# Two attentions on one core: row sums by eight products with ones, held sums, a warmed array, and f and g through seven exp tiles

## The chip, the cores and the metric

The kernel runs on one core of one Trainium2 chip. The metric is the device time in microseconds (us) of a whole execution. The engines are TensorE (PE in the profile; PEld is its weight load), VectorE (DVE), ScalarE (ACT), GpSimd (POOL) and SyncE (SP, which here only issues DMAs). Runs of one kernel agree within 0.14% (the widest spread is that of run 8, 2987.79 to 2991.91 us). All runs below are of the fast state.

A ratio below is the mean time of one kernel's fast runs over that of the other's of the same rounds, so it is not quite the ratio of the medians that are quoted.

## The reference, cut to what matters

Two layers over x of shape 8 x 64 x 64 x 64, that is eight images of 64 channels and 4096 positions:

```python
# layer 0 ("first kind" below)
f = Wf x + bf            # 8 channels
g = Wg x + bg            # 8 channels
h = Wh x + bh            # 64 channels
s = f^T g                # 4096 x 4096 scores of each image
x = x + h softmax(s)^T
# layer 1 ("second kind" below)
xn = group_norm(x)       # 8 groups
q, k, v = Wqkv xn + bqkv
out = Wp (softmax(q k^T / 8) v) + bp + x
```

## The kernel before

The kernel computes exp of the scores without a maximum, multiplies by the values, and divides by the row sums at the end. Each image and kind has four chunks of 512 columns for each half of the positions. Each chunk has 16 steps. A step makes four score banks, takes exp of them into one tile `e` of 128 x 2048, multiplies it with the values (`weigh`), and adds it on VectorE to the chunk's sum tile `esum`. The order is: first kind of image 0, first kind of image 1, second kind of image 0, first kind of image 2, second kind of image 1, and so on. So the run begins with eight chunks of the first kind in a row.

The sum tile has two halves `esum[:, 0]` and `esum[:, 1]`, and what is summed over the 128 partitions is their total. It is closed in one of two ways:

```python
        def holds(self, c):
            return self.kind == 0 and self.b > 0 and c < (1 if self.b == 1 else NC - 1)
...
            def halves():
                if other is not None:
                    vector.tensor_add(raw, raw, other)
                vector.tensor_add(esum[:, 0], esum[:, 0], esum[:, 1])

            def transposed():      # the way of "held" chunks: VectorE sums over partitions
                ...
                vector.tensor_reduce(part, esum[:, 0].rearrange(...), axis=AX.X,
                                     op=ALU.add, apply_transpose=True)
                ...
            def sums(spare):       # the other way: products with ones on TensorE
                for h in range(2):
                    for i in range(2):
                        row = 32 * (2 * h + i)
                        matmul(z[row : row + 32, 0:width], ones[:, 0:32],
                               esum[:, 0, h, ts(i, width)],
                               start=True, stop=True, tile_position=(0, row))
...
        held = at.holds(c)
        if at.kind == 1 or next_kind == 1 or held:
            when = now + 4
            if at.kind == 0:
                when = (i // NC + 1) * NC * NT + 1 + 3 * c     # inside the second kind
            for s, u in ((0, halves), (1, transposed), (5, reciprocals), (8, result)):
                at_step(when + s, behind(u), 0)
            return
        behind(halves)()
        ...
        at_step(now + delay, lambda: sums(spare), BANK)
```

f and g of the first kind are split into a high and a low part through two tiles, `full` and `high`, of which there is one each (`bufs=1` in the pool `work`). The exp tiles come from a pool of six:

```python
    ppool = ctx.enter_context(tc.tile_pool(name="ppool", bufs=6))
...
            full = work.tile([P, 2, CW], F32, tag="full", bufs=1, name=f"full_{n}")
            nc.scalar.activation(full[rows], ps[rows], AF.Identity, bias=fgb[rows, :])
            high = work.tile([P, 2, CW], F32R, tag="high", bufs=1, name=f"high_{n}")
            vector.tensor_copy(high[rows], full[rows])          # the cast
            ...                                                 # subtraction, then DMAs read high
```

Of the kernel before, what the change touches and what calls it, by code (L numbers as in the profile page):

```python
# [9 lines left out]
F32 = mybir.dt.float32  # L10
# [58 lines left out]
def fast_path(  # L69
# [28 lines left out]
    const = ctx.enter_context(tc.tile_pool(name="const", bufs=1))  # L98
    xpool = ctx.enter_context(tc.tile_pool(name="xpool", bufs=3))
    proj = ctx.enter_context(tc.tile_pool(name="proj", bufs=1))  # L100
    ppool = ctx.enter_context(tc.tile_pool(name="ppool", bufs=6))
    work = ctx.enter_context(tc.tile_pool(name="work", bufs=2))
    small = ctx.enter_context(tc.tile_pool(name="small", bufs=2))
    dram = ctx.enter_context(tc.tile_pool(name="dram", bufs=1, space=bass.MemoryType.DRAM))
# [16 lines left out]

    made_last = {}
    added = None
    tight = False

    def in_order(made, engine="tensor"):

# [22 lines left out]
    def matmul(*args, **kwargs):  # L150
        in_order(nc.tensor.matmul(*args, **kwargs))  # L151

    def behind(work_):


        def made():
            with tc.issue_after(added):
                work_()

        return made  # L160
# [22 lines left out]
        return t  # L183


    w1 = const.tile([P, 2, C8], F32, name="w1")
    for i, (w, queue) in enumerate(((WfT, nc.scalar), (WgT, nc.sync))):
        for h in range(2):
# [24 lines left out]
    with tc.issue_after(masked):  # L213
# [10 lines left out]
        wfg = const.tile([P, 2, 4, C8], F32, name="wfg")  # L224
        nc.vector.tensor_copy(wfg, w1.unsqueeze(2).broadcast_to([P, 2, 4, C8]))
    wfg = wfg.rearrange("p i s c -> p (i s c)")
    fgb_low = const.tile([P, 2], F32, name="fgb_low")
    fgb, lowmask = fgb_low[:, 0:1], fgb_low[:, 1:2]
    for j in range(2):
# [20 lines left out]
    nc.vector.tensor_single_scalar(odd, lane, 1, op=ALU.bitwise_and)  # L250
    lowmask32 = const.tile([P, 1], F32, name="lowmask32")
    nc.vector.tensor_scalar(lowmask32, odd, -1.0, None, op0=ALU.mult)
    ones = const.tile([P, C], F32, name="ones")
    nc.vector.memset(ones, 1.0)


    QP = 2 * CW // P
# [67 lines left out]
    class Attention:  # L325
# [7 lines left out]

        def holds(self, c):

            return self.kind == 0 and self.b > 0 and c < (1 if self.b == 1 else NC - 1)

        def values(self, src, w, c):

            ps = pair()  # L340
            for t in range(TPC):
                for m in range(2):
                    for h in range(2):
                        matmul(
                            ps[ts(m, C), h, ts(t, C)], src[ts(h, C), ds(t * P + m * C, C)],
                            w[ts(h, C), :], start=True, stop=True,
                        )

            copy = vector.tensor_copy if self.kind == self.b == c == 0 else nc.scalar.copy
            copy(  # L350
                self.vt[:, :, ts(c, TPC), :],
                ps[:, :, 0 : TPC * C].rearrange("k p (t c) -> k p t c", c=C),
            )

        def finish(self, acc, esum, c, index):

            n = f"{self.name}_{c}"
            raw = work.tile([P, CW], F32, tag="raw", bufs=4, name=f"raw_{n}")
            other = self.total(raw, acc, index)
            zt = small.tile([P, QP], F32, tag="zt", bufs=4, name=f"zt_{n}")  # L360
            width = CW // 2
            r = four = None
# [6 lines that stand above are left out]
            def transposed():  # L369


                nonlocal four
                both_ = work.tile([P, 8 * QP], F32, tag="zs", name=f"part_{n}")
                part = both_[:, 0:32]
                four = both_[:, 32:].rearrange("p (a k) -> p a k", k=QP)
                vector.tensor_reduce(
                    part, esum[:, 0].rearrange("p h (i b) -> p b (h i)", b=32),
                    axis=AX.X, op=ALU.add, apply_transpose=True,
                )
                for a in range(4):  # L380
                    nc.sync.dma_start(four[:, a, :], part[ts(a, 32), :])

            def sums(spare):

                z = banks[:, spare, :]

                zs = work.tile([P, width], F32, tag="zs", name=f"zs_{n}")
                for h in range(2):
                    for i in range(2):
                        row = 32 * (2 * h + i)  # L390
                        matmul(
                            z[row : row + 32, 0:width], ones[:, 0:32], esum[:, 0, h, ts(i, width)],
                            start=True, stop=True, tile_position=(0, row),
                        )
                nc.scalar.copy(zs, z[:, 0:width])
                for h in range(2):
                    for i in range(2):
                        row = 32 * (2 * h + i)
                        nc.sync.dma_start(zt[row : row + 32, :], zs[row : row + 1, :])  # L399

            def broadcast():
                nonlocal r
                r = work.tile([P, CW], F32, tag="r", name=f"r_{n}")

            def reciprocals():
                rt = stash[:, ts(index, QP)]
                if four is not None:
                    vector.tensor_reduce(
                        zt, four.rearrange("p a k -> p k a"), axis=AX.X, op=ALU.add
                    )  # L410
                vector.reciprocal(rt, zt)
                broadcast()
                dealt = recips[index]
                nc.sync.dma_start(dealt, rt)
                for h in range(2):
                    row = dealt[ts(h, C), :].rearrange("p e -> (p e)")
                    nc.sync.dma_start(r[ts(h, C), :], row.partition_broadcast(C))

            def result():
                vector.tensor_mul(raw, raw, r)  # L420
                self.residual(raw, c)

            return halves, transposed, sums, reciprocals, result
# [52 lines left out]
    class Layer0(Attention):  # L476
# [4 lines left out]
        def before(self):  # L481
# [24 lines left out]
                        load_x(b)  # L506

            if self.b == 0:
                return [(-1, begin, True), (0, rest, True)] + [
                    (  # L510
                        (-1, 1, 5, 8)[c],
                        lambda c=c: self.values(x_tiles[0][:, ts(c, CW)], wh, c),
                        True,
                    )
                    for c in range(NC)
                ]
# [16 lines left out]
        def home(self, c):  # L533

            if self.b > 1:
                if c == 0:
                    layers1[self.b].own(F32)
                return layers1[self.b].parts[:, c, :]
            layers0[2].own_vt()
            return layers0[2].vt.rearrange("q p t c -> q (p t c)")  # L540

        def project_direct(self):

            ps = pair()
            full = work.tile([P, 2, CW], F32, tag="full", bufs=1, name="full_direct")
            high = work.tile([P, 2, CW], F32R, tag="high", bufs=1, name="high_direct")
            for i, dst in enumerate((self.f, self.g)):
                matmul(
                    ps[:, i, :], direct[:, i, :], x_tiles[self.b][:, 0:CW], start=True, stop=True
                )  # L550
                nc.scalar.activation(
                    full[:, i, :], ps[:, i, :], AF.Identity, bias=bias2[:, i : i + 1]
                )
                vector.tensor_copy(high[:, i, :], full[:, i, :])
                vector.scalar_tensor_tensor(
                    dst[:, 0:CW], high[:, i, :].bitcast(F32), lowmask2[:, i : i + 1],
                    full[:, i, :], op0=ALU.mult, op1=ALU.add,
                )

        def project(self, k, js=(0, 1)):  # L560
# [4 lines left out]
            for j in js:  # L565
                for h in range(2):
# [1 line left out]
                        ps[ts(j, C), h, :], wfg[ts(h, C), :], xt[ts(h, C), ts(2 * k + j, CW)],  # L568
                        start=True, stop=True,
                    )  # L570
            full = work.tile([P, 2, CW], F32, tag="full", bufs=1, name=f"full_{n}")
            rows = slice(js[0] * C, P)
            nc.scalar.activation(full[rows], ps[rows], AF.Identity, bias=fgb[rows, :])  # L573
            high = work.tile([P, 2, CW], F32R, tag="high", bufs=1, name=f"high_{n}")
            vector.tensor_copy(high[rows], full[rows])

            split = high
# [16 lines left out]
        def project_all(self):  # L594
# [6 lines left out]
            for c in range(NC):  # L601
                for h in range(2):
# [1 line left out]
                        ps[ts(c, 32), h, :], wfg32[ts(h, C), :], xt[ts(h, C), ts(c, CW)],  # L604
                        start=True, stop=True, tile_position=(h * C, 32 * c),
                    )
            full = work.tile([P, 2, CW], F32, tag="full", bufs=1, name=f"full_{n}")
            nc.scalar.activation(full, ps, AF.Identity, bias=fgb32)
            high = work.tile([P, 2, CW], F32R, tag="high", bufs=1, name=f"high_{n}")
            vector.tensor_copy(high, full)  # L610
            split = high
            vector.scalar_tensor_tensor(
# [46 lines left out]
    class Layer1(Attention):  # L659
# [8 lines left out]
        def before(self):  # L668
# [32 lines left out]
            def deviations():  # L701
# [8 lines left out]
                )  # L710
                y = guess.bitcast(F32)
                w = small.tile([P, 1], F32, tag="w", name=f"w_{n}")
                for i in range(4):
                    vector.scalar_tensor_tensor(w, y, y, ve, op0=ALU.mult, op1=ALU.mult)
                    vector.tensor_scalar(w, w, -0.5, 1.5, op0=ALU.mult, op1=ALU.add)
                    vector.tensor_mul(y, y, w)
# [179 lines left out]
    def finished(i, now):  # L896
# [7 lines left out]
        if at.kind == 1 or next_kind == 1 or held:  # L904
# [4 lines left out]
            for s, u in ((0, halves), (1, transposed), (5, reciprocals), (8, result)):  # L909
                at_step(when + s, behind(u), 0)  # L910
            return
        behind(halves)()

        spare = outer[c % 2 if at.kind == 0 else 1]
        delay = 7 if at.kind == 0 else 5
# [499 lines left out]
```

## Time and profile before

| | before |
|---|---|
| median of the first three runs | 3005.96 us |
| span of the profiled run | 3004.0 us |
| TensorE busy | 2973.7 us |
| VectorE busy, 90 to 338 us | 236.46 of 248 us |
| first scores of the second kind start at | 338.95 us |
| one period (one image's first and second kind) after that | 368.5 us |

The prediction shows the lines. The busy time of TensorE is the row to start with: what a change can take out without removing matmul work is the 30 us in which it is idle, and the time that a slow clock adds to its busy time. The busy time doesn't show the second part: the granted clock was 0.75 at 14 to 16 us, 0.50 at 16 to 24 and 0.69 at 24 to 26, as much as some 10 us at 0.50, which by an estimate from these numbers is 5 us of busy time. The second row to look at is the stretch of the eight first chunks, in which VectorE is nearly full as well.

### The profile page before, as it was taken

Reading aid. Unit: us, or ns where it says so; the run is one execution under the profiler, and the core shown is the slowest. Engines: PE = TensorE matmul, PEld = TensorE weight load, DVE = VectorE, ACT = ScalarE, POOL = GpSimd, SP = SyncE. Lnnn points to the kernel's source line nnn. Section 1 sums busy time; section 2 is a strip of 40 time slices with the busy share of each in tenths; the row PEclk is TensorE's granted clock in tenths of the full one; section 3 lists DMA queues with packets and bytes.
Section 4 is the critical chain, followed back from the end, with each engine's and each line's share of the span. In section 5 each row is a group of like instructions: output and inputs, shape, how many; then the busy total and the mean of one; then the engine's idle time right before and its main releaser. Section 6 shows DMA issues by size and latency. Waiting matters only on the chain.

```text
span 3004.0 us, 58286 instructions
## 1 busy us (share of the span) xinstructions
PE 2973.7 (99%) x25629; PEld 1078.7 (36%) x25629; DVE 2574.0 (86%) x1659; ACT 2073.0 (69%) x2019; POOL 16.1 (1%) x40
## 2 busy tenths in 40 slices
PE   8999999999999999999999999999999999999998
PEld 3333333333333333333333333333333333333333
DVE  7999986899878998789986999879997799976776
ACT  6888656786567866678666785668856688566554
POOL 2000000000000000000000000000000000000000
PEclk9999999999999999999999999999999999999999
DMA  2100100101001010010100102000020000000000
GB/s 65 43 8 15 47 16 19 30 1 44 20 20 29 1 45 19 21 28 1 49 19 20 26 1 51 16 23 22 1 52 20 19 8 1 17 24 15 9 16 13
DMA packets 77141, 66.93 MB, mean 22 GB/s; under 512 B 54048, under 2 KB 54080, under 8 KB 75088
## 3 DMA queue, kind: packets, MB, share of 16 engines
q1 hardware_dynamic: 75792, 63.01, 8.7%
q8 instruction: 202, 3.31, 0.5%
q14 instruction: 59, 0.48, 0.1%
q0 software_dynamic: 768, 0.09, 0.0%
q10 hardware_dynamic: 320, 0.04, 0.0%
HBM read 39.84 MB, written 12.32 MB: 17 GB/s over the span
## 4 chain that ended last, share of the span: by engine, by line
PE 93%; DVE 4%; issue 1%; ACT 1%; DMA 0%; SPq 0%; DVEq 0%; ACTq 0%
PE banks L151 93%; DVE esum_l L141 3%; DVE vt_l L141 1%; ACT e_l L1013 1%; DMA x<-in_x_dram 0%; DVE x L141 0%; DVE raw_l L141 0%; DVE st_l L141 0%; ACT full_l L573 0%; DVE high_l L141 0%; DVE kq_l L141 0%; DVE rt L141 0%; SPq L399 0%; DMA zt_l<-zs_l 0%; DVE w_l L141 0%
## 5 line engine op out<-in xcount | busy, mean ns | idle before, releaser
L141 DVE TENSOR_TENSOR esum_l<-esum_l,e_l 128x2048 f32<-128x2048 f32 x629 | 1438.9, 2288 | 272.0 <-ACT e_l L972 246.3
L972 ACT ACTIVATE e_l<-banks 128x1024 f32<-128x1024 f32 x1024 | 992.2, 1022 | 680.6 <-PE banks L151 680.6
L151 PE MATMUL banks<-e_l,v_l 64*64 64x512 f32 (+1 forms) x8780 | 1090.2, 586 | 0.0
L1013 ACT ACTIVATE e_l<-banks 128x2048 f32<-128x2048 f32 (+3 forms) x727 | 953.8, 1373 | 183.5 <-PE banks L151 165.9
L151 PE MATMUL banks<-kq_l 64*64 64x512 f32 (+1 forms) x8448 | 1004.4, 585 | 6.5 <-ACT e_l L1013 5.7
L151 PE MATMUL banks<-e_l,vt_l 128*64 128x512 f32 (+1 forms) x4056 | 829.8, 550 | 0.0
L141 DVE TENSOR_TENSOR kq_l<-kq_l,e_l 128x2048 f32<-128x2048 f32 x252 | 577.5, 2292 | 24.4 <-ACT e_l L1013 0.5
L151 PEld LDWEIGHTS banks<-e_l,v_l 64*64 64x64 f32 (+1 forms) x8780 | 346.9, 133 | 589.3 <-issue 490.0
L151 PEld LDWEIGHTS banks<-kq_l 64*64 64x64 f32 (+1 forms) x8448 | 326.2, 134 | 602.9 <-issue 561.8
L151 PEld LDWEIGHTS banks<-e_l,vt_l 128*64 128x64 f32 x4056 | 267.8, 136 | 467.7 <-issue 447.6
L151 PE MATMUL banks<-fg_l 32*128 32x512 f32 x1792 | 204.7, 459 | 6.2 <-ACT e_l L1013 3.1
L141 DVE TENSOR_TENSOR esum_l<-e_l,e_l 128x2048 f32<-128x2048 f32 x45 | 102.3, 2274 | 86.2 <-ACT e_l L972 86.2
L151 PEld LDWEIGHTS banks<-fg_l 32*128 32x128 f32 x1792 | 84.8, 183 | 186.8 <-ACT e_l L1013 139.8
L141 DVE TRANSPOSE_TENSOR_REDUCE part_l<-esum_l 128x32 f32<-128x1024 f32 x38 | 74.7, 1967 | 0.0
L141 DVE TENSOR_TENSOR esum_l<-esum_l 128x1024 f32<-128x1024 f32 x44 | 53.7, 1220 | 0.4
L141 DVE TENSOR_TENSOR raw_l<-raw_l,r_l 128x512 f32<-128x512 f32 x63 | 43.2, 685 | 2.1 <-DMA r_l<-recips 2.1
L141 DVE TENSOR_TENSOR kq_l<-e_l,e_l 128x2048 f32<-128x2048 f32 x18 | 41.1, 2283 | 0.0
L651 ACT COPY raw_l<-banks 128x512 f32<-128x512 f32 x32 | 18.9, 590 | 25.2 <-PE banks L151 24.3
L141 DVE TRANSPOSE_TENSOR_REDUCE part_l<-kq_l 128x32 f32<-128x1024 f32 x18 | 35.2, 1955 | 0.0
L141 DVE TENSOR_TENSOR vt_l<-vt_l,e_l 128x2048 f32<-128x2048 f32 x14 | 32.1, 2291 | 1.2
L764 ACT ACTIVATE kq_l<-banks,kqb 64x256 f32<-64x256 f32 x64 | 30.1, 470 | 1.2
L151 PEld LDWEIGHTS banks<-wh,x 64*64 64x64 f32 x1024 | 21.2, 138 | 16.7 <-issue 15.8
(127 smaller groups left out, 467.9 us busy)
## 6 DMA issues: line engine op xcount, KB each, us to landing
r_l<-recips SPq DMA_DIRECT2D x126, 128.0 KB
kq_l<-kq_l SPq DMA_DIRECT2D x64, 128.0 KB
out_dram<-raw_l SPq DMA_DIRECT2D x62, 128.0 KB
x<-in_x_dram SPq DMA_DIRECT2D x30, 256.0 KB
fg_l<-fg_sent_l SPq DMA_DIRECT2D x24, 256.0 KB
fg_l<-fg_sent_l SPq DMA_DIRECT2D x48, 128.0 KB
part_l<-part_l SPq DMA_DIRECT2D x228, 4.0 KB
fg_sent_l<-high_l SPq DMA_DIRECT2D x28, 128.0 KB
```

The source lines that it names most:

```text
L141: it = getattr(nc.vector, name)(*args, **kwargs)
L151: in_order(nc.tensor.matmul(*args, **kwargs))
L651: nc.scalar.copy(raw, acc[0])
L764: nc.scalar.activation(self.q[ts(h, C), cols[1]], ps[other, 1, 0:width], AF.Identity, bias=k1["kqb"][other, :],)
L972: nc.scalar.activation(e[:, p], both_ps[p], AF.Exp, scale=at.scale)
L1013: nc.scalar.activation(e.rearrange("k p h n -> k (p h) n")[:, first_ : first_ + n_, :], banks[:, bank : bank + n_, :], AF.Exp, scale=at.scale,
```

## The change

The intent is to take work from VectorE in the first eight chunks, to take waits out of the first 30 us, and to start with the array at full clock:

- `holds`: two more chunks of image 1 are held; their sums are closed inside the second kind.
- `sums`: the two halves are no longer added on VectorE; eight products with ones accumulate both.
- `full` and `high` come from the exp pool, which grows from six to seven tiles.
- 18 and 10 products that do nothing are made at the very start, before x lands.
- The second projection of image 0 comes at step 2 instead of 0, the first copy of values goes to ScalarE, VectorE's order is held from the beginning, and the inverse root takes three Newton rounds instead of four.

The diff, cut to its core:

```diff
-    ppool = ctx.enter_context(tc.tile_pool(name="ppool", bufs=6))
+    ppool = ctx.enter_context(tc.tile_pool(name="ppool", bufs=7))
...
-    tight = False
+    tight = True
...
+    def warm(rows, n):
+        for i in range(n):
+            matmul(banks[0:C, 7, 0:C], rows, rows, start=True, stop=True)
+
+    warm(ones, 18)
...
+    warm(wfg, 10)
...
-            return self.kind == 0 and self.b > 0 and c < (1 if self.b == 1 else NC - 1)
+            return self.kind == 0 and self.b > 0 and c < NC - 1
...
-            copy = vector.tensor_copy if self.kind == self.b == c == 0 else nc.scalar.copy
-            copy(
+            nc.scalar.copy(
...
+                for p in range(2):
                     for h in range(2):
                         for i in range(2):
                             row = 32 * (2 * h + i)
                             matmul(
                                 z[row : row + 32, 0:width], ones[:, 0:32],
-                                esum[:, 0, h, ts(i, width)],
-                                start=True, stop=True, tile_position=(0, row),
+                                esum[:, p, h, ts(i, width)],
+                                start=p == 0, stop=p == 1, tile_position=(0, row),
                             )
...
-                return [(-1, begin, True), (0, rest, True)] + [
+                return [(-1, begin, True), (2, rest, True)] + [
...
+            if c == 1:
+                self.free = proj.tile([P, 2, NH], F32, tag="fg", name="free")
+            return self.free[:, c - 1, :]
...
-            full = work.tile([P, 2, CW], F32, tag="full", bufs=1, name=f"full_{n}")
+            full = ppool.tile([P, 2, 2, CW], F32, tag="e", name=f"full_{n}")[:, 0]
-            high = work.tile([P, 2, CW], F32R, tag="high", bufs=1, name=f"high_{n}")
+            high = ppool.tile([P, 2, 2, CW], F32R, tag="e", name=f"high_{n}")[:, 0]
...
-                for i in range(4):
+                for i in range(3):
...
-        behind(halves)()
```

More of the change, by code (lines that the diff above doesn't have):

```diff
@@ L183, in twice @@
         return t
+    ones = const.tile([P, C], F32, name="ones")
+    nc.vector.memset(ones, 1.0)
+    def warm(rows, n):
+        for i in range(n):
+            matmul(banks[0:C, 7, 0:C], rows, rows, start=True, stop=True)
+    warm(ones, 18)
     w1 = const.tile([P, 2, C8], F32, name="w1")
@@ L252, in fast_path @@
     nc.vector.tensor_scalar(lowmask32, odd, -1.0, None, op0=ALU.mult)
-    ones = const.tile([P, C], F32, name="ones")
-    nc.vector.memset(ones, 1.0)
     QP = 2 * CW // P
@@ L387, in sums @@
                 zs = work.tile([P, width], F32, tag="zs", name=f"zs_{n}")
-                for h in range(2):
-                    for i in range(2):
-                        row = 32 * (2 * h + i)
-                        matmul(
-                            z[row : row + 32, 0:width], ones[:, 0:32], esum[:, 0, h, ts(i, width)],
-                            start=True, stop=True, tile_position=(0, row),
-                        )
+                for p in range(2):
+                    for h in range(2):
+                        for i in range(2):
+                            row = 32 * (2 * h + i)
+                            matmul(
+                                z[row : row + 32, 0:width], ones[:, 0:32],
+                                esum[:, p, h, ts(i, width)],
+                                start=p == 0, stop=p == 1, tile_position=(0, row),
+                            )
                 nc.scalar.copy(zs, z[:, 0:width])
@@ L538, in home @@
                 return layers1[self.b].parts[:, c, :]
-            layers0[2].own_vt()
-            return layers0[2].vt.rearrange("q p t c -> q (p t c)")
+            if c == 0:
+                layers0[2].own_vt()
+                return layers0[2].vt.rearrange("q p t c -> q (p t c)")
+            if c == 1:
+                self.free = proj.tile([P, 2, NH], F32, tag="fg", name="free")
+            return self.free[:, c - 1, :]
         def project_direct(self):
             ps = pair()
-            full = work.tile([P, 2, CW], F32, tag="full", bufs=1, name="full_direct")
-            high = work.tile([P, 2, CW], F32R, tag="high", bufs=1, name="high_direct")
+            full = ppool.tile([P, 2, 2, CW], F32, tag="e", name="full_direct")[:, 0]
+            high = ppool.tile([P, 2, 2, CW], F32R, tag="e", name="high_direct")[:, 0]
             for i, dst in enumerate((self.f, self.g)):
@@ L606, in project_all @@
                     )
-            full = work.tile([P, 2, CW], F32, tag="full", bufs=1, name=f"full_{n}")
+            full = ppool.tile([P, 2, 2, CW], F32, tag="e", name=f"full_{n}")[:, 0]
             nc.scalar.activation(full, ps, AF.Identity, bias=fgb32)
-            high = work.tile([P, 2, CW], F32R, tag="high", bufs=1, name=f"high_{n}")
+            high = ppool.tile([P, 2, 2, CW], F32R, tag="e", name=f"high_{n}")[:, 0]
             vector.tensor_copy(high, full)
```

## The prediction

> **What bounds the kernel now.** I read the page's first part, then the table of busy time by stretches, then the chain that ended last in order of time, then the waits, and last the timeline of the first 30 us.
>
> ```profile
> PE 2973.7 (99%) x25629; PEld 1078.7 (36%) x25629; DVE 2574.0 (86%) x1659; ACT 2073.0 (69%) x2019; POOL 16.1 (1%) x40
> ```
>
> TensorE is busy for 2973.7 of 3004.0 us. All of its idle time is 30.3 us, 1.0% of the span, so a change that removes no matmul work can win at most about that. Where is it? In the stretches (columns: length, then busy time of PE, PEld, DVE, ACT, POOL, then granted clock):
>
> ```profile
> core 0: us, PE busy (x) PEld busy (x) DVE busy (x) ACT busy (x) POOL busy (x), PEclk, DMA share, GB/s
> 0.00:28.00 28.00, 17.71 (x115) 6.30 (x115) 9.61 (x25) 11.95 (x10) 16.14 (x40) 0.82 0.27 61
> 28.00:90.00 62.00, 61.68 (x449) 23.43 (x449) 56.20 (x27) 51.37 (x52) 0.00 (x0) 1.00 0.23 56
> 90.00:338.00 248.00, 239.14 (x1640) 86.38 (x1644) 236.46 (x147) 199.03 (x175) 0.00 (x0) 1.00 0.08 21
> 338.00:564.00 226.00, 226.00 (x2350) 83.41 (x2354) 177.49 (x130) 138.31 (x157) 0.00 (x0) 1.00 0.11 28
> 564.00:932.00 368.00, 367.59 (x3188) 133.42 (x3184) 321.63 (x207) 257.34 (x250) 0.00 (x0) 1.00 0.10 23
> ```
>
> The first 28 us hold 10.3 us of idle PE at a mean clock of 0.82; 90 to 338 us hold 8.9 us, with VectorE at 95% (236.46 of 248); the last 12 us hold 8.4 us. From 338 us on PE has no hole: 226.00 of 226, then 0.4 us in each period of 368 us. The chain says so too:
>
> ```profile
> 313.63 249.57 PE banks L151 x2510
> ...
> 566.06 365.62 PE banks L151 x3137
> ```
>
> 338 us is where the second kind of attention starts (its first score matmuls are at 338.95 us). Before it lie eight chunks of the first kind, 16 steps each. The waits that VectorE causes in that stretch (28 to 338 us) are these:
>
> ```profile
> ACT e_l L1013 <- DVE esum_l L141: 11.4, 12, 4.1
> ...
> ACT e_l L1013 <- DVE vt_l L141: 3.7, 3, 1.6
> ```
>
> ScalarE waited 15.1 us for a tile of exp that VectorE had not yet added. In the whole trace these sums are the same, so no later stage waits for such a tile. Last the start:
>
> ```profile
> 7.26 3.75 PE L151 MATMUL banks<-x,direct 128*128 128x512 f32 x4 [7.26 <-DMA x<-in_x_dram]
> ...
> 20.59 3.68 PE L151 MATMUL banks<-e_l,vt_l 128*64 128x512 f32 x8
> ...
> 25.33 1.94 PE L151 MATMUL banks<-e_l,vt_l 128*64 128x512 f32 x8
> 25.34 0.69 DVE L141 CAST high_l<-full_l 128x1024 fp32r<-128x1024 f32 x1 [7.75 <-DMA fg_l<-high_l]
> ...
> 27.28 2.28 DVE L141 TENSOR_TENSOR esum_l<-e_l,e_l 128x2048 f32<-128x2048 f32 x1
> ```
>
> Eight matmuls take 3.68 us at 20.59 and 1.94 us at 25.33: half clock until about 25 us. The cast at 25.34 waited 7.75 us because the only "high" tile was still being read by eight DMAs; the first add stands behind it in order and runs at 27.28, though its two exps were done at 21.25.
>
> [...] The products with ones use four column tiles; their eight instructions took 0.64 us together at 75.61 us, though each is listed at 390 ns[...].
>
> **The change, part by part.** The VectorE rows concerned:
>
> ```profile
> L141 DVE TENSOR_TENSOR esum_l<-esum_l 128x1024 f32<-128x1024 f32 x44 | 53.7, 1220 | 0.4
> ...
> L141 DVE TENSOR_TENSOR raw_l<-raw_l,r_l 128x512 f32<-128x512 f32 x63 | 43.2, 685 | 2.1 <-DMA r_l<-recips 2.1
> ```
>
> Start. Warm-up products should bring full clock by about 7.3 us. The direct products then take 1.9 instead of 3.7 us. ScalarE and VectorE follow: first f at 8.4, second at 9.15, then cast and subtraction (0.43 + 0.75 each) until about 11.7 instead of 14.26 us (the copy of 0.69 us that stood between goes to ScalarE). Scores start at 11.7 instead of 14.4. With a pool of seven tiles the second cast no longer waits for DMAs: exp 0 at 12.5 to 14.4, exp 1 to about 16.8, the projection's activation to 18, cast and subtraction (0.69 + 1.28) to 20, first add at 20 instead of 27.28: 7 us earlier. PE's fourth round of scores (27.2 to 28.3 us now) should be at about 21.5: it needs the first eight DMAs, which land 7.7 us after the subtraction (17.6 to 25.3 now, so 13.8 to 21.5). Start: 6 us gained.
>
> VectorE up to 338 us. Gone: six halves of a measured pitch of 1.15 us (6.9 us; four are dropped, two moved behind 338), one result (multiply, residual, statistics: 2.2 us) and two reciprocals moved behind (0.3), one Newton round (0.6). That is 10 us, on top of the start of 7 us. In-order waits of VectorE at 81, 87 and 283 us (1.3, 2.2 and 2.7 us) may shrink by 3 us. VectorE alone would reach the state it now has at 338 us at 338 - 7 - 10 - 3 = 318.
>
> TensorE up to 338 us. Adding PE's gaps between 28 and 338 us in its timeline (0.61, 0.86, 0.74, 1.11, 0.85, 0.60, 1.14, 1.21, 0.61, 0.48 and four of about 0.3) gives 9.5 us; scores stretched from 0.73 to 0.97 us and split rounds add about 3.5: 13 us at most from missing tiles. New: four sums have 16 instructions for 8, an estimate of 0.43 us each (256 columns, half of the 0.43 us that a pair of 512 columns takes, twice), 1.7 us; two sums go (0.57 us beside other work, 1.1 us). So PE alone would be there at 338 - 6 - 13 + 0.6 = 320.
>
> Both engines end within 2 us of each other[...]; I add 2 us: 322, a gain of 16 us. A seventh tile lets VectorE lag one step more, which helps both.
>
> After 338 us. Two held chunks bring 1.22 + 1.96 + 0.2 us each, and with what else moved, VectorE gets about 9 us more in the first 14 steps of the second kind. There a step takes PE 3.43 us (score matmuls at 719.50 and 722.93 us) and VectorE's add 2.39 us; 14 steps leave VectorE 15 us, and it now spends those on such deferred work. Nine more put it four steps further behind, on a lag of two at 338 us (counted from exps and adds in the windows): six of seven tiles, so hidden by a narrow margin, and caught up some 20 steps later. PE's work there doesn't change. Newton's fourth round in the other seven images (0.6 us each) is beside PE: nothing. The projections of later images take two of the seven exp tiles for some 10 us at the same place; VectorE lags three or four tiles then (256 exps against 253 steps added at 705 us), so one or two are free at once: nothing, or half a us each. Tail: unchanged. Sum: 3006 - 16 = 2990 us.
>
> **Rivals.** (1) PE is the bound throughout and what VectorE gives is not on its path: rounds between 28 and 90 us already run at the full pace (a round of seven banks each 3.83 us), and there VectorE has slack. Then only the start counts: about 3000. For it speaks 99% of PE busy; against it, 15.1 us of waits for tiles. (2) The warm-up overruns: 28 products of 128x64 by 64 columns are 56 instructions if each is two, as the others here are. An eighth of 512 columns would be 0.11 us at half clock, in all 6 us, just the time between ones (0.9) and x (7.26). If the weight load (0.2 us at half clock) is not hidden in one tile, it is some 15 us, x waits till about 16 us, and the start loses 6 to 9: about 3000 to 3006. (3) Tiles become scarcer: full and high for later images take tiles from exp at each change to the second kind. If VectorE lags four there, ScalarE stalls up to 2.4 us in each of six images: 15 us back, about 3004. Against it: from 705 to 708 us PE is still at old weighings, and two more tiles come free. (4) Waits at the start move: the shared SP queue makes its 24 DMAs at 0.82 us each; if step 8 comes before its slices have landed, 2 to 4 us of the start are lost.
>
> **Range and chances.** The two terms are 6 (2 to 8) and 10 (4 to 12); both low gives 3000, both high 2986, and the start may beat my estimate by a few us. Range 2982 to 3000. 2% are 60 us, twice all of PE's idle time: faster by over 2% is nearly excluded; slower by 60 us would need a stall in each period of 368 us, which no view suggests.
>
> **What would show it.** Right: the granted clock in the first 28 us well over 0.9; the first add at about 20 us; first scores of the second kind at about 322 instead of 338.95; ScalarE's waits for sums down from 15.1 us to below 6; six halves fewer by this time; periods of 368 us as before. Wrong: x's first product later than 7.5 us (rival 2); new waits of the activation of full for VectorE or DMA at each change of kind, or a longer period (rival 3); 338.95 moved by the start's 6 us only (rival 1).

## The result, and the profile after

The changed kernel took 2989.03 us (median of 4 runs, 2989.01 to 2990.43) against 3005.99 us (4 runs). The ratio is 0.9945, with a 95% interval of 0.9928 to 0.9962. That is a gain of 17 us, where 16 were forecast.

First the engines' row of the page, then the same stretches as before, moved by what had been gained at their edges:

```profile
PE 2969.8 (99%) x25693; PEld 1081.5 (36%) x25693; DVE 2567.6 (86%) x1634; ACT 2072.3 (69%) x2019; POOL 16.3 (1%) x40
```

```profile
core 0: us, PE busy (x) PEld busy (x) DVE busy (x) ACT busy (x) POOL busy (x), PEclk, DMA share, GB/s
0.00:28.00 28.00, 23.29 (x235) 12.44 (x235) 16.18 (x27) 19.04 (x17) 16.34 (x40) 1.00 0.37 88
21.00:83.00 62.00, 61.63 (x452) 23.60 (x455) 53.93 (x26) 51.29 (x51) 0.00 (x0) 1.00 0.24 56
83.00:321.00 238.00, 236.24 (x1648) 85.54 (x1646) 228.87 (x136) 198.73 (x175) 0.00 (x0) 1.00 0.08 20
321.00:547.00 226.00, 226.00 (x2340) 83.44 (x2340) 183.76 (x137) 137.24 (x156) 0.00 (x0) 1.00 0.12 30
547.00:915.00 368.00, 367.59 (x3188) 133.38 (x3184) 321.16 (x204) 257.34 (x250) 0.00 (x0) 1.00 0.10 23
```

The shares of the whole span have hardly moved (PE 99%, DVE 86% in both kernels), although 17 us are gone. The stretches show where. In the first 28 us VectorE does 16.18 us of work instead of 9.61. The stretch that took 248 us takes 238: TensorE has 1.8 us of idle time in it instead of 8.9, and 236.24 us of busy time instead of 239.14. The next 226 and the 368 us after them are as before; only VectorE's busy time rose by 6.3 us in the 226 (177.49 to 183.76), which is the work that was moved there (the forecast was about 9). The chain that ended last says the same of the long stretches:

```profile
297.95 248.34 PE banks L151 x2488
...
549.15 365.63 PE banks L151 x3137
```

These two start 15.7 and 16.9 us earlier than the pieces shown of before; from the second on the distance is constant. Five marks in the two timelines divide the gain:

| mark | before | after | gained |
|---|---|---|---|
| first product with x | 7.26 us | 7.30 us | 0.0 |
| exp of step 0 | 16.37 us | 12.19 us | 4.2 |
| scores just ahead of image 0's last piece of values | 38.89 us | 31.92 us | 7.0 |
| first scores of the second kind | 338.95 us | 322.04 us | 16.9 |
| end of the span | 3004.0 us | 2987.1 us | 16.9 |

So 7.0 us come from the start and 9.9 us from the rest of the first eight chunks. The start, in the timeline of the changed kernel (start, duration, engine, line, operation):

```profile
1.07 4.10 PE L151 MATMUL banks<-ones 128*64 128x64 f32 x36 [1.07 <-DVE ones L187]
...
7.30 1.96 PE L151 MATMUL banks<-x,direct 128*128 128x512 f32 x4 [0.63 <-DMA x<-in_x_dram]
...
17.73 0.69 DVE L141 CAST high_l<-full_l 128x1024 fp32r<-128x1024 f32 x1 [4.11 <-ACT full_l L586]
18.09 6.59 ACT L1025 ACTIVATE e_l<-banks 128x2048 f32<-128x2048 f32 x5 [0.39 <-ACT full_l L586]
...
18.18 1.94 PE L151 MATMUL banks<-e_l,vt_l 128*64 128x512 f32 x8
...
19.66 2.29 DVE L141 TENSOR_TENSOR esum_l<-e_l,e_l 128x2048 f32<-128x2048 f32 x1
```

The first products take 1.96 instead of 3.75 us, the cast waits for ScalarE and no longer for DMAs, and the first add comes 7.6 us earlier. The waits of ScalarE's exp, over the whole trace:

```profile
ACT e_l L984 <- issue: 9.1, 6, 1.5
...
ACT e_l L984 <- DMA fg_l<-fg_sent_l: 3.0, 2, 1.5
...
ACT e_l L1025 <- DVE free L141: 1.7, 1, 1.7
```

The last row is all that remains of the 15.1 us of waits for VectorE (`free` is the new sum tile). The first two rows are new. In the exp of the second kind (L984), eight waits of at most 1.5 us are put down to "issue" and to the DMAs of f and g. The two kernels' groups show that exp's wait for PE fell from 680.6 to 668.9 us at the same time, a fall of 11.7 us against 12.1 us of new waits. TensorE has no hole there and the period is still 368.50 us (549.15 to 917.65), so these waits only took the place of a wait that was there anyway.

VectorE's adds of halves:

```profile
L141 DVE TENSOR_TENSOR esum_l<-esum_l 128x1024 f32<-128x1024 f32 x38 | 46.3, 1219 | 0.2
```

There are 38 instead of 44. Two of the six are now listed under `free`, inside the second kind; four are gone.

### The profile page after: what moved, and what is told of

Its sections match the earlier page's. It is cut to its first block, busy times and chain, and to the rows that moved or that the text cites. A ratio compares the mean times of both kernels' runs of the same rounds, so it can differ in the third digit from the quotient of the medians.

```text
span 2987.1 us, 58391 instructions
## 1 busy us (share of the span) xinstructions
PE 2969.8 (99%) x25693; PEld 1081.5 (36%) x25693; DVE 2567.6 (86%) x1634; ACT 2072.3 (69%) x2019; POOL 16.3 (1%) x40
## 4 chain that ended last, share of the span: by engine, by line
PE 95%; DVE 3%; issue 1%; ACT 1%; DMA 0%; SPq 0%; DVEq 0%; ACTq 0%
PE banks L151 95%; DVE vt_l L141 1%; DVE esum_l L141 1%; DVE free L141 1%; ACT e_l L1025 0%; DMA x<-in_x_dram 0%; ACT kq_l L777 0%; DVE rt L141 0%; DVE x L141 0%; SPq L198 0%; DVE raw_l L141 0%; DVE raw_end L141 0%; DVE st_l L141 0%; DVE w_l L141 0%; ACT full_l L586 0%
## 5 line engine op out<-in xcount | busy, mean ns | idle before, releaser
L141 DVE TENSOR_TENSOR esum_l<-esum_l,e_l 128x2048 f32<-128x2048 f32 x601 | 1374.5, 2287 | 269.2 <-ACT e_l L984 246.7
L984 ACT ACTIVATE e_l<-banks 128x1024 f32<-128x1024 f32 x1024 | 992.3, 1022 | 681.1 <-PE banks L151 668.9
L141 DVE TENSOR_TENSOR free<-free,e_l 128x2048 f32<-128x2048 f32 x28 | 64.2, 2291 | 2.6
L141 DVE TENSOR_TENSOR esum_l<-esum_l 128x1024 f32<-128x1024 f32 x38 | 46.3, 1219 | 0.2
```

Source lines behind the costliest of these rows:

```text
L141: it = getattr(nc.vector, name)(*args, **kwargs)
L984: nc.scalar.activation(e[:, p], both_ps[p], AF.Exp, scale=at.scale)
```

## The experiments

All were timed in five rounds beside the kernel before, which took 3005.2 to 3006.0 us (medians). Twelve kernels ran.

**1. The start alone.** The changed kernel with `sums`, `holds` and the Newton rounds of before:

```diff
-            return self.kind == 0 and self.b > 0 and c < NC - 1
+            return self.kind == 0 and self.b > 0 and c < (1 if self.b == 1 else NC - 1)
-                for p in range(2):                      # in sums; start/stop True
+                for p in range(1):
+        behind(halves)()
-                for i in range(3):                      # Newton
+                for i in range(4):
```

> The kernel before with the start's parts alone (warm-up products, f and g through exp tiles of which there are seven, second projection at step 2, the first copy on ScalarE, order held from the beginning); the sums are as before: six halves on VectorE, one chunk held, four products, four Newton rounds. My theory: the start gives 7 of the 17 us, relief of VectorE the other 10, so 2999 us, the first add at about 19.7 us and the first scores of the second kind at about 332 us; the seventh tile may give 1 to 2 us of the 10 here already. Rival (the start and the seventh tile do it all, TensorE being the bound): 2989 to 2991 us.

It took 2998.71 us (2997.51 to 3000.6), ratio 0.9974, and the first scores of the second kind came at 331.86 us, 7.1 earlier than before. VectorE's waits are still there:

```profile
ACT e_l L1026 <- DVE esum_l L141: 6.8, 6, 2.3
...
ACT e_l L1026 <- DVE vt_l L141: 3.8, 3, 2.0
```

So the start is worth 7.3 us and the relief of VectorE the other 10. The rival by which the start and the seventh tile do it all has fallen. What the seventh tile brought here can't be told, since the array fell to half rate twice in this profile, from 216 and from 305 us, for 3.4 us each time (the mean granted clock is 0.97 from 200 to 250 us and from 300 to 350, and 1.00 from 250 to 300). Each time it followed a wait for a tile of exp (1.45 and 1.57 us):

```profile
305.37 1.05 PE L151 MATMUL banks<-kq_l,wkq_wvp 64*64 64x256 f32 x8 [1.57 <-ACT e_l L1026]
306.35 3.63 PE L151 MATMUL banks<-e_l,v_l 128*64 128x512 f32 x12
```

At a granted clock of 1.00 the same groups take 0.66 and 2.37 us (run 3, at 234.75 and 235.34 us). So the second fall made them 1.65 us longer, and the two falls cost some 3.3 us by an estimate from this; the profile of before has none from 26 us until its last 15 us (granted clock 1.00). So part of the 10 us that the relief is worth over this kernel is such falls.

**2. No warm-up.**

```diff
-    warm(ones, 18)
-    warm(wfg, 10)
```

> The changed kernel without its 28 warm-up products. If the clock is on the path of the start: half rate until about 20 us, the first products 3.7 instead of 2.0 us, exp 0 some 1.7 us later, 2991 to 2993 us. Rival (the start hangs on ScalarE, VectorE and DMAs, not on the clock): less than 0.7 us lost.

It took 2991.2 us (2990.93 to 2993.14), 2.2 us more than 2989.0. The first scores of the second kind came at 324.04, 2.0 us later.

```profile
7.25 3.39 PE L151 MATMUL banks<-x,direct 128*128 128x512 f32 x4 [7.25 <-DMA x<-in_x_dram]
10.56 0.65 PE L151 MATMUL banks<-x,wfg 64*64 64x512 f32 x2
```

The clock is on the path, but not for the reason that the expectation gives. Without warm-up the first products are slow (3.39 us), and the very next ones are at full rate (0.65 us, as in the changed kernel at 9.19 us). The array was up at about 10.5 us, and stayed up in this run. (The granted clock is recorded as 1.00 over the first 28 us here too, so that sign of the prediction does not tell a warm start from a cold one.) What was lost is the 1.4 us of the first products, and two short waits (0.38 and 0.62 us at 22.2 and 23.3 us) for the DMAs of f and g, which left later.

**3. Six exp tiles.**

```diff
-    ppool = ctx.enter_context(tc.tile_pool(name="ppool", bufs=7))
+    ppool = ctx.enter_context(tc.tile_pool(name="ppool", bufs=6))
```

> The changed kernel with six exp tiles. If the seventh tile is what lets VectorE lag behind TensorE: 1 to 4 us lost, ScalarE waits for VectorE's sums again for 5 us or more. If not: within 0.5 us of 2989.0.

It took 2993.96 us (2993.18 to 2994.51): 4.9 us lost, more than forecast. ScalarE waited 4.8 us for VectorE, in four waits of up to 3.5 us, and the first scores of the second kind came at 326.25, 4.2 us later. The granted clock (the third number from the end) tells the rest:

```profile
240.00:242.00 2.00, 1.48 (x3) 0.56 (x3) 1.90 (x2) 1.94 (x4) 0.00 (x0) 0.87 0.00 0
242.00:244.00 2.00, 2.00 (x9) 1.00 (x10) 2.00 (x1) 2.00 (x2) 0.00 (x0) 0.50 0.00 0
244.00:246.00 2.00, 2.00 (x8) 0.52 (x7) 1.90 (x2) 0.56 (x1) 0.00 (x0) 0.77 0.00 0
```

After holes of 1.21, 0.61 and 0.49 us within 4 us, the array ran at half rate for about 3.4 us (an estimate from the clock in these rows). A wait for VectorE here costs its length and then a slow stretch as well: the 16 products at 242.01 us took 4.64 us, where 16 took 3.23 at 230.37.

**4. f and g in tiles of their own.** Own tiles and seven exp tiles do not fit: the build of both stopped with the message that the pool `work` wants 38 KB in a partition, with 31.9 left. So this is with six.

```diff
-            full = ppool.tile([P, 2, 2, CW], F32, tag="e", name=f"full_{n}")[:, 0]
+            full = work.tile([P, 2, CW], F32, tag="full", bufs=1, name=f"full_{n}")
-            high = ppool.tile([P, 2, 2, CW], F32R, tag="e", name=f"high_{n}")[:, 0]
+            high = work.tile([P, 2, CW], F32R, tag="high", bufs=1, name=f"high_{n}")
-    ... bufs=7      # the exp pool
+    ... bufs=6
```

> The changed kernel with full and high in their own single tiles again and six exp tiles (seven and their own tiles do not fit together). The second cast waits again for the eight DMAs that read high: it should run at about 21.4 instead of 17.7 us, the first add at 23.3 instead of 19.7. Theory: 3 to 4 us lost by this, plus what six tiles for seven cost (its own run): 2993 to 2996 us. Rival (the cast's wait is beside TensorE's work and only VectorE's lag takes it): no more than the run with six tiles alone.

It took 2997.35 us (2996.16 to 2997.74): 3.4 us more than six tiles alone. The cast waited 7.56 us for the DMAs again and ran at 22.48, the first add at 24.41 us. Both times are 1.1 us later than forecast. The loss is as the theory says, but its cause is not shown, because the clock fell here too, to half from about 14 to 21 us (0.52, 0.50, 0.50 and 0.77 in the four stretches of 2 us from 14 to 22):

```profile
15.95 1.98 PE L151 MATMUL banks<-x,wfg 64*64 64x512 f32 x8
17.86 3.43 PE L151 MATMUL banks<-e_l,vt_l 128*64 128x512 f32 x8
```

With six tiles alone (run 3) the same groups take 1.09 and 1.94 us. That is 2.4 of the 3.5 us by which the scores ahead of image 0's last piece of values come later (35.62 for 32.11). The other 1.1 us were lost before (scores at 15.22 for 14.16): ScalarE could write `full` only after VectorE had left the single tile. So the rival, that the cast's wait lies beside TensorE's work, still stands for these 3.5 us. Whether the single tiles bring the fall on is open; run 7 shows it without them.

**5. Halves on VectorE.**

```diff
-                for p in range(2):                      # in sums; start/stop True
+                for p in range(1):
+        behind(halves)()
```

> The changed kernel with the halves of the first four chunks added on VectorE again (1.15 us each, 4.6 us in all) and four products with ones for eight (TensorE gains 1.7 us). If VectorE's work is on the path of the first eight chunks: 2 to 4.6 us lost, so 2991 to 2993.6. If TensorE alone bounds them: 1.7 us gained, 2987.3.

It took 2992.39 us (2992.1 to 2995.5), 3.4 us more; the second kind's first scores at 325.34. VectorE's work is on the path, though TensorE was given 1.7 us of its own work back. With TensorE alone as bound it would have been faster. Here too the loss has two parts: at 215.37 us TensorE had waited 1.45 us for exp, and then ran 3.4 us at half rate, in which 16 products took 4.92 instead of 3.23 us (the mean granted clock is 0.97 from 200 to 250 us).

**6. One chunk held, as before.**

```diff
-            return self.kind == 0 and self.b > 0 and c < NC - 1
+            return self.kind == 0 and self.b > 0 and c < (1 if self.b == 1 else NC - 1)
```

> The changed kernel with only one chunk of the second image held, as before; the other two take the products with ones. VectorE gets one result and two reciprocals more before the second kind starts (2.6 us), TensorE two products of 1.07 us and rounds narrower by a bank. Theory: 2 to 4 us lost, 2991 to 2993. Rival (moved work is paid where it goes, so holding wins nothing): within 0.7 us of 2989.0.

It took 2991.94 us (2991.82 to 2993.68), 2.9 us more; first scores at 324.84. So what is moved into the second kind is not paid there.

**7. VectorE relieved further, with wrong sums.**

```diff
-        else:
+        elif not (i < 2 * NC and t in (5, 11)):
             added = vector.tensor_add(esum, first if t == 1 else esum, e).ins
```

> Wrong sums on purpose: two of the fifteen adds of each of the first eight chunks are left out, 16 x 2.39 = 38 us of VectorE. It shows how much VectorE still costs in the changed kernel. Theory: TensorE's gaps that remain before 322 us are 1.7 us plus 1.3 us of stretched scores, so 2 to 4 us gained, 2985 to 2987, and no more. Rival (VectorE is still the bound there): 10 us or more gained.

The sums are wrong as intended (relative error 0.20). The time was 2989.92 us (2987.06 to 2990.31), so the median was no gain at all. The profile shows what happened. First TensorE, then the stretches:

```profile
14.81 1.99 PE L151 MATMUL banks<-x,wfg 64*64 64x512 f32 x8
16.73 3.68 PE L151 MATMUL banks<-e_l,vt_l 128*64 128x512 f32 x8
```

```profile
12.00:14.00 2.00, 0.80 (x36) 0.56 (x32) 1.46 (x2) 1.91 (x3) 1.90 (x5) 0.96 0.05 8
14.00:16.00 2.00, 1.92 (x12) 0.60 (x12) 0.00 (x0) 1.57 (x3) 1.99 (x6) 0.50 0.32 98
```

The array fell to half rate at about 14 us and came back near 21 (0.50 until 20 us, 0.83 at 20 to 22), with the same start as the changed kernel, in whose profile the same two groups take 1.09 and 1.94 us. That put all that follows 3.0 us later (scores at 31.09 instead of 28.09). From there to the second kind it took 292.07 us (31.09 to 323.16) against 293.95 (28.09 to 322.04): 1.9 us less, and TensorE has no gap from 25 us on. The single runs agree: the four at 2989.09 to 2990.31 us have a mean clock of 0.998, the one at 2987.06 has 0.999. So 38 us less on VectorE win 1.9 us. The rival has fallen: VectorE hardly bounds this stretch any more, TensorE does.

**8. x first.**

```diff
-    for i, (w, queue) in enumerate(((WfT, nc.scalar), (WgT, nc.sync))):
+    for i, (w, queue) in enumerate(((WfT, nc.scalar), (WgT, nc.gpsimd))):
```

> The changed kernel with Wg loaded from the GpSimd queue, so that x's first piece leaves the SP queue 1.5 us earlier. The first product waits for x at 7.30 us now; it should run at about 5.9 us, and all that follows 1.4 us earlier: 2987.6 us. Rival (the copies of the weights into their block layout, done at 5.85 us, or Wg itself, come later and take its place): within 0.5 us of 2989.0.

2988.79 us (2987.79 to 2991.91), which is unclear by its spread. Its profiled run took 2987.79. In it the first product ran at 6.43 us, straight behind the last warm-up product: the ten products on `wfg` now stood in its way. Of the 0.8 us won at the start (27.29 instead of 28.09), 0.47 were left at the second kind (321.57). The rest went into the largest hole: TensorE waited 1.58 instead of 1.22 us for VectorE's normalised columns.

**9. The changed kernel again**, unaltered, to see its spread.

> The changed kernel once more, unaltered, to see how often the clock falls in its start. In the profile of the run with two adds left out the array was at half rate from about 14 to 20 us with the same start, which put the fourth round of scores 3.0 us later. Theory: the single runs fall in two groups, most at 2989.0, some 1 to 3 us above. Rival (the dip belongs to that kernel): all within 0.3 us of 2989.0.

Runs of 2989.11, 2988.8, 2991.69, 2990.25 and 2990.4 us: two groups. With the four runs of the result, five of nine lie between 2988.8 and 2989.1, four are 1.2 to 2.7 us above 2989.0.

**10. Fillers.**

```diff
-                ]
+                ] + [(-1, lambda: warm(ones, 7), 0), (1, lambda: warm(ones, 9), 0)]
```

> The changed kernel with 16 more products that do nothing, in the two holes of TensorE of 0.9 and 1.3 us at 10.7 and 12.9 us. If the clock falls because TensorE is thinly used between 9 and 14 us, it stays up: no run over 2990, median 2989.0. If the fall does not hang on this: the same spread as the changed kernel. If the fillers stand in the way of the scores: the scores later than 11.7 and 14.2 us and up to 1 us lost.

All five runs lie between 2988.86 and 2989.11 us, median 2988.93. The upper group is gone and nothing is lost: scores at 11.68 and 14.16 us. That the upper group is the fall of the clock at 14 us is argued and not shown: no run of the upper group of the changed kernel itself has a profile here, and five runs against four of nine are few. The recorded mean clock speaks for it in one run only: it is 0.998 for 2991.69 us and 0.999 for the other eight runs. A fall as long as that of run 7 takes 0.001 off the mean, by an estimate from the clock of its stretches (3.4 us lost from 12 to 22 us, of 2988); one of half that length could hide in the rounding.

**11. Later projections.**

```diff
-                s = 31 + 8 * c if self.b == 0 else 35 + 7 * c
+                s = 33 + 8 * c if self.b == 0 else 35 + 7 * c
-                    (s - 4, behind(lambda c=c: normal(c)), False),
+                    (s - (6 if self.b == 0 else 4), behind(lambda c=c: normal(c)), False),
```

> The changed kernel with the projections of the first image's second kind two steps later, behind the same work of VectorE. The largest hole left in TensorE before 322 us (1.22 us at 234.55 us, waiting for VectorE's normalised columns) should close: 0.8 to 1.7 us gained, first scores of the second kind at 320.5 to 321.2 instead of 322.04 us. Rival (VectorE's lag is the bound there, so the hole moves elsewhere): within 0.3 us.

2989.49 us (2988.99 to 2990.82), first scores at 322.39: no gain. The hole for the normalised columns closed, and one of 1.39 us opened at 238.34, where TensorE waits for exp; ScalarE's waits for `free` rose from 1.7 to 3.2 us. The wait changed its name, as the rival says.

**12. Together:** fillers, later projections, x first, and four products on `wfg` instead of ten.

> Fillers, the later projections, and x first with four products on wfg for ten (with ten, the warm-up itself held the first product until 6.43 us). First product at about 5.95 us; 1.35 us from the start and 0.8 to 1.7 us from the projections: 2985.9 to 2986.9 us. Rival (what the start wins is given back while VectorE bounds the first chunks, as with x first alone, where 0.83 us at the start left 0.47 us at the second kind): 2987.5 us or more.

2987.6 us (2987.5 to 2988.68), ratio 0.9942 to before. It beats both kernels, the changed one by 1.4 us of its lower group. The first product ran at 5.48 us, 1.28 us were won by the scores at 26.81, and 0.64 were left at the second kind (321.40): the rival's case, by a hair.

## Why the prediction was right

**Where the gain lies.** The step that bounded everything was TensorE's idle time: 10.3 us in the first 28 and 8.9 us in 90 to 338. (The prediction calls all idle time, 30 us, the most that can be won. That leaves out busy time at half rate, which its own part on the start counts on winning.) Measured: 16.9 us came from before 338.95 us and none from after it. The rival that only the start counts fell in run 1, which stopped at 2998.71.

**The start.** The chain was right piece by piece: scores at 11.64 (11.7 forecast), exp 0 at 12.19 (12.5), first add at 19.66 (20). It gave 7.0 us rather than 6: I took the fourth round to wait for the DMAs until 21.5, but its first four units ran at 20.05 and the rest at 21.37. What was wrong in it was a reading, not a sum. "Half clock until about 25 us" is not what happened before. Its granted clock (third number from the end) is 1.00 at 10 to 14 us, 0.75 at 14 to 16 and 0.50 at 16 to 24:

```profile
12.00:14.00 2.00, 0.79 (x26) 0.49 (x22) 1.36 (x3) 0.00 (x0) 1.89 (x6) 1.00 0.02 0
14.00:16.00 2.00, 0.96 (x4) 0.50 (x4) 0.74 (x2) 1.11 (x1) 2.00 (x4) 0.75 0.11 32
16.00:18.00 2.00, 2.00 (x10) 0.30 (x8) 1.49 (x2) 1.63 (x1) 2.00 (x5) 0.50 0.05 9
```

Run 2 shows that the array came up at 10.5 us without warm-up (3.39 us for the first four products, 0.65 for the next two). That 28 products would bring full clock by 7.3 us was my estimate; measured, the first four took 1.96 us at 7.30. In the kernel before, the array was slow (3.75 us for the first four), rose (0.59 us for two at 11.73, where two take 0.60 in the changed kernel), and fell again at about 15 us. This fall did not come back in the changed kernel's profile, and that was in part luck: 4.2 of the start's 7.0 us are won by exp 0 and 2.8 behind it, where run 7, with the same start and the fall, loses 3.0. Nothing in the prediction provided against a second fall. Of single parts, only the warm-up was measured (2.2 us). The 3.4 us of run 4 contain a fall of the clock, so the share of the tiles of f and g, and that of order, copy and step 2, stay open.

**VectorE up to the second kind.** Ten us were worked out and 9.9 measured. The gain is 7.1 us of idle time and 2.9 us of busy time of TensorE, where the prediction had at most 9.5 and 3.5. Taken out one at a time, the halves cost 3.4, the held chunks 2.9 and the seventh tile 4.9 us. These are not parts of one sum, for the first and the last include a fall of the clock of about 1.7 us each (estimated as half of 3.4 us at half rate). That the tile is worth more once both engines are close, because it then takes up short differences between them, is argued and not shown.

**TensorE's new work.** The estimate of 0.43 us for eight more product instructions holds: 16 took 1.07 us at each of four places where 8 had taken 0.64.

**After 338 us.** That the moved work is hidden held. Its size was off: 6.3 us more for VectorE, not 9, and a lag of two to three tiles until 350 us, not six. So the margin was wider than forecast.

**The other rivals.** The warm-up did not overrun: 36 instructions took 4.10 us and 20 took 1.65, 0.08 to 0.11 us each, and x was still waited for by 0.63 us. It does overrun once x comes earlier (run 8). Scarce tiles at the changes of kind do make new waits of ScalarE, 12.1 us in all, but on a wait that was there. Of DMAs that come too late only run 2 shows a trace, 1.0 us.

**The residue.** I added 2 us for two engines so close together, as a guess. Run 7 measures it as 1.9 us for this one pair.

## What to carry to other kernels

When the bound engine is busy for 99%, add up its idle time by stretch before anything else, and the time that it ran at half clock: together they are the ceiling, and they tell in which stage to work. Where two engines run level, relief of one is worth what it takes until the other one bounds, and here that was 10 of the first 10 us and 1.9 of the next 38. A wait of TensorE can cost more than its length: in runs 1, 3 and 5 waits of 1.2 to 1.6 us were followed by 3.4 us at half rate, some 1.7 us more (1.65 in run 1, 1.69 in run 5). Before a change of a microsecond is judged, look at the single runs and at the granted clock in the first 30 us, and see whether a filler makes the runs agree.

## What the runs show of TensorE's clock

- The array fell at about 14 us after waits of 0.92 and 1.27 us, with TensorE busy for 1.88 of the 4 us from 10 to 14 (run 7), and at 241 us after holes of 1.21, 0.61 and 0.49 us (run 3). Waits of 1.58 us (run 8, 12 products behind it in 2.37 us) and 1.39 us (run 11, 16 products behind it in 3.2 us) passed without a fall, so the longest wait alone does not decide it. The changed kernel was busy for 1.93 us from 10 to 14, with waits of 0.91 and 1.26 us, and its profile has a granted clock of 1.00 throughout the first 28 us.
- The start varies from run to run: in run 7, 2.0 to 3.3 us lie between the one run with a mean clock of 0.999 and the four with 0.998. That the spread of 1.2 to 2.7 us of the changed kernel is the same thing is not shown; it was gone in five runs with 16 idle products in the holes.
- The granted clock did not show the cold start, and the durations did: before's record says 1.00 from the first microsecond until 14 us, while the first four products took 3.75 us against 1.96 in the changed kernel.
- The cost of such a warm-up in fp32: 36 instructions of 128x64 by 64 columns took 4.10 us from 1.07 us on (0.11 us each; 3.56 us in run 4), the next 20 took 1.65 us (0.08).
